# A hand-written list scheduler is given new costs: measured occupancies, a first-come port, banks chosen by the plan, single score and value tiles

## The chip, the cores and the metric

The kernel runs on one core of one Trainium2 chip. The metric is the device time of one execution in microseconds. A core has five engines with queues of their own: PE (matmuls; the profile shows its weight loads as PEld), DVE (VectorE), ACT (ScalarE), POOL (GpSimd) and SP (SyncE, here only for DMAs). Each runs its own instructions strictly in the order in which the program issues them, and waits on semaphores for the others.

## The reference

Sixteen graphs (batches) of 1024 nodes with 256 features go through two layers; the same 0/1 adjacency masks both.

```python
def _L0_gnn_ref(features, adj, Wq, Wk, Wv, Wffn, g1, b1, g2, b2):
    q, k, v = heads(features @ Wq), heads(features @ Wk), heads(features @ Wv)   # 8 heads of 32
    e = jnp.einsum('whqd,whkd->whqk', q, k)
    e = jnp.where(e >= 0, e, ALPHA * e)
    attn = jax.nn.softmax(jnp.where(adj[:, None] > 0, e, NEG), axis=-1)
    h = jnp.einsum('whqk,whkd->whqd', attn, v)
    ...
    out = _layernorm(h, g1, b1)
    out = jnp.concatenate([out, features], axis=-1) @ Wffn.T
    return _layernorm(out, g2, b2) + features

def _gat(h, adj, W, a, out_features):                                            # twice in layer 1
    Wh = jnp.matmul(h, W)
    e = leaky_relu(Wh @ a[:out_features] + swapaxes(Wh @ a[out_features:], 1, 2))
    att = jax.nn.softmax(jnp.where(adj > 0, e, NEG), axis=1)
    return jnp.matmul(att, Wh)
...
    h = _layernorm(residual + _gat(_gat(x, ...), ...), g_ln1, b_ln1)
    ff = relu(h @ w_ff1 + b_ff1) @ w_ff2 + b_ff2                                 # 256 -> 1024 -> 256
    return _layernorm(h + ff, g_ln2, b_ln2)
```

## The kernel before

For each batch b the work has three kinds of parts, and parts of neighbouring batches run beside each other.

**Preparing batch b+1** (`project`): x is loaded and transposed (L355), the adjacency is turned into an 8-bit mask by DVE (L412), transposed (L422) and copied (L426); q and k of two groups of four heads are made as products L475, which ACT copies out rounded (L478, "high") and DVE as the remainder (L480, "low"); both go to DRAM and come back stacked for each head (L568). The values are products L507, copied out at L514 or L516.

**The heads** (`all_scores`, `weights`, `all_values`): for each of 8 heads and 8 key tiles, two matmuls (L601) make a 128 x 1024 score tile in two PSUM banks. ACT scales it (L619), DVE takes the maximum (L621) and so frees the score banks, ACT takes the exponential (L624), POOL multiplies with the mask (L628). The result p, one of five buffers, is multiplied with the values (L650), two halves of 512 columns beside each other on 33 (or 64) columns of the array. For b > 0 the score matmuls of two key tiles are issued together and both score tiles are taken first; the value matmuls of two key tiles (GV = 2) are always issued as one group, after which both p are given back.

**The rest of batch b** (`rest`): normalisations, the projection (L753, L756), rows of the first graph layer (L785), the attention matrix of 8 tiles on DVE (L838, L841), its product with the rows (L876), the second layer's attention and product (L901, with residual by L929), and the feed-forward part (L941, L969).

PSUM has eight banks: four for two score tiles, one for the values' sum, and three for all other products ("misc", `ps_m`). The misc tiles have one tag with three buffers, so the framework hands the banks out in rotation; a product waits for the one made three before it.

**The order** of all instructions is made when the kernel is built, by class `Order` (L35 to L175). Every part above is a generator. It yields `on(ENGINE=cost, ...)` before it issues an instruction, `take` and `give` for buffers, `wait` and `fire` for data, and `aim` for the time at which it should run. `run` keeps a clock for each engine and issues, among those that could start at most WINDOW = 300 ns after the earliest, the one with the lowest aim. A cost with two engines goes to the one that ends first. An operation marked `shared` on DVE or POOL also waits for the common SBUF port. After an operation the thread is ready HOP later (60 to 100 ns), except on the same engine. Matmuls run at half speed in the plan in a stretch of 3413 ns after one that was less than 43% busy. The plan's pools are counted, not numbered: it takes whichever misc bank is free first. Aims are shares of SLOT = 253 us after a batch's start; the constants are in `AIM` (batches from 2 on) and `EARLY` (0 and 1). None of the costs is read by the chip; only the order of the instructions, and which of two engines does a copy, come out of them.

Of the kernel before, what the change touches and what calls it, by code (L numbers as in the profile page):

```python
# [34 lines left out]
class Order:  # L35
# [5 lines left out]

    HOP = dict(PE=100.0, ACT=70.0, DVE=60.0, POOL=70.0, SP=60.0)
    WINDOW = 300.0

# [3 lines left out]
    def __init__(self, **pools):  # L54
        self.clock = defaultdict(float)
        self.port = 0.0
        self.transfers = 0.0
        self.stretch, self.done, self.half = 0, 0.0, True
        self.pools = {k: [0.0] * n for k, n in pools.items()}
        self.queues = defaultdict(list)  # L60
        self.events = {}
        self.waiting = defaultdict(list)
        self.active = []
        self.made = 0
        self.now = 0.0
        self.busy = defaultdict(float)

    def add(self, thread, aim, ready=0.0):
        self.made += 1
        self.step({"gen": thread, "aim": aim, "no": self.made, "ready": ready}, None)  # L70

    def step(self, th, sent):
        while True:
# [19 lines left out]
            elif what == "take":  # L93
                if not self.pools[arg]:
                    self.queues[arg].append(th)
                    return
                th["ready"] = max(th["ready"], self.pools[arg].pop(0))
            elif what == "give":
                queue = self.queues[arg]
                if queue:  # L100
                    other = min(queue, key=lambda o: (o["aim"], o["no"]))
                    queue.remove(other)
                    other["ready"] = max(other["ready"], th["ready"])
                    self.step(other, None)
                else:
                    self.pools[arg].append(th["ready"])
                    self.pools[arg].sort()
            elif what == "start":
                self.add(arg[0], arg[1], th["ready"])
            elif what == "pause":  # L110
                th["ready"] += arg
            elif what == "aim":
                th["aim"] = arg[0]
                th["ready"] = max(th["ready"], arg[0] - arg[1])
# [19 lines left out]
    def run(self):  # L134
        while self.active:
            could = []
            for th in self.active:
                costs, shared, delay = th["op"]
                best = None
                for engine, cost in costs.items():  # L140
                    ready = th["ready"]
                    if th.get("last", ())[:2] == (engine, ready):
                        ready -= self.HOP[engine]
                    t = max(self.clock[engine], ready)
                    if shared and engine in ("DVE", "POOL"):
                        t = max(t, self.port)
                    if best is None or t + cost < best[0] + best[2]:
                        best = t, engine, cost
                could.append((best, th))
            first = min(c[0][0] for c in could)  # L150
            (t, engine, cost), th = min((c for c in could if c[0][0] <= first + self.WINDOW),
                                        key=lambda c: (c[1]["aim"], c[1]["no"]))
            if th["op"][1] and engine in ("DVE", "POOL"):

                lead = 100.0 if engine == "DVE" else -100.0
                before = [c for c in could if c[1]["op"][1] and c[0][1] in ("DVE", "POOL")
                          and c[0][1] != engine and c[0][0] + lead < t]
                if before:
                    (t, engine, cost), th = min(before, key=lambda c: (c[1]["aim"], c[1]["no"]))
            costs, shared, delay = th["op"]  # L160
            self.active.remove(th)
            end = self.clock[engine] = self.end(engine, t, cost)
# [4 lines left out]
            th["ready"] = end + self.HOP[engine]  # L167
# [10 lines left out]
def on(shared=False, delay=0.0, **costs):  # L178
    return "on", (costs, shared, delay)
# [45 lines left out]
def unshifted_path(  # L225
# [28 lines left out]
    AIM = dict(mask0=0.759, x=0.818, x_step=0, mask=0.747, mask_step=0.0264, qk0=0.614, qk1=0.898,  # L254
               qk_step=0.0231, v0=0.832, v1=0.974, v_step=0.0591, rows=-0.244, rows_step=0.0408, first0=0.12,
               first1=0.252, graph0=-0.009, graph1=0.21, graph_step=0, second=0.355, second_step=0.0335,
               normed=0.78, normed_step=0.026, ff_wait=(None, 0, 1, 0), ff=(0.532, -0.011, 0.487, 0.497),
               ff_step=0.0386, fast0=0.425, fast1=0.938, fast15=0.832, lead=3.15)

    EARLY = dict(x=0.87, x_step=0.005, mask=0.747, mask_step=0.0296, qk0=0.692, qk1=0.909, qk_step=0.0345,  # L260
                 v0=0.774, v1=1.001, v_step=0.0568, rows=-0.139, rows_step=0.0071, first0=0.082, first1=-0.169,
                 graph0=-0.195, graph1=-0.027, graph_step=0, second=0.302, second_step=0.0335, normed=0.781,
# [14 lines left out]
    def misc(dtype=FT):  # L277
        return psum.tile([P, HALF], dtype, tag="misc", name="ps_m", bufs=bufs["misc"])
# [36 lines left out]
    def evacuate(n):  # L315
        return on(DVE=140 + 1.06 * n, ACT=150 + 0.87 * n)

    def evacuate_by(n):

        return on(DVE=190 + 1.06 * n, ACT=250 + 0.87 * n)  # L320
# [5 lines left out]
    def stats(srcs):  # L326
# [3 lines left out]
        for i, src in enumerate(srcs):  # L330
            st = small.tile([P, 6], FT, name="st")
            yield on(DVE=420)
            nc.vector.bn_stats(st, src)
            yield on(DVE=185)
            nc.vector.bn_aggr(mv[:, i, :], st)  # L335
        rs = small.tile([P, n], FT, name=f"rs{n}")
        yield on(POOL=260)
        nc.gpsimd.tensor_scalar(rs, mv[:, :, 1], EPS, None, op0=OP.add)  # L338
        yield on(POOL=450 + 150 * n, shared=True)
# [3 lines left out]
    def normalized(dst, srcs, mv, rs):  # L343
        for i, (row, src) in enumerate(zip(dst, srcs)):
            if row is src:
                yield on(DVE=340, shared=True)
            else:
                yield on(DVE=440)
# [38 lines left out]
    def mask_part(b, t, halves):  # L387
# [22 lines left out]
        for i, ai in enumerate(ints):  # L410
            yield on(DVE=440, shared=True)
# [8 lines left out]
        yield on(PE=90 + 112 * n)  # L420
# [3 lines left out]
        yield on(ACT=150 + 225 * n)  # L424
# [19 lines left out]
    def x_pair(b, u):  # L444
# [7 lines left out]
        yield on(PE=450)  # L452
# [7 lines left out]
    def qk_part(b, g, o, nh):  # L460
# [12 lines left out]
        yield on(PE=1720)  # L473
# [3 lines left out]
        yield on(ACT=590)  # L477
        nc.scalar.copy(high.bitcast(FR), pa)  # L478
        yield on(DVE=690)
# [20 lines left out]
    def v_part(b, g, u):  # L500
# [3 lines left out]
        yield on(PE=1000)  # L504
# [15 lines left out]
    def project_v(b, g, t0):  # L520
# [3 lines left out]
        yield on(POOL=500)  # L524
# [56 lines left out]
    def all_scores():  # L581
        for b in range(B):
# [4 lines left out]
            for h in range(H):  # L587
                yield wait(("stack", b, h))
                q, kk = stacks[b, h]
                n = 2 if b else 1  # L590
                for t in range(0, NT, n):
                    due = t0 + (h * NT + t) / 2 * pace(b)
                    yield aim(due, AIM["lead"] * PACE)
                    for _ in range(n):
                        yield take("scores")
                    ps = [psum.tile([P, N], FT, tag="scores", name="ps_s") for _ in range(n)]
                    yield on(PE=450 * n)
                    for i in range(n):
                        for nh in range(NH):
                            cols = slice(nh * HALF, (nh + 1) * HALF)  # L600
                            nc.tensor.matmul(ps[i][:, cols], kk[:, (t + i) * P:(t + i + 1) * P], q[:, cols],  # L601
                                             start=True, stop=True)
                    if t + n == NT:
                        yield give("stacks")
                    for i in range(n):
                        yield start(weights(b, h, t + i, ps[i]), due + i * PACE / 2)

    def weights(b, h, t, ps):
# [3 lines left out]
        if b == 0:  # L612
            engine = yield on(ACT=1050, DVE=1230)
        else:
            engine = yield on(ACT=1050)
# [4 lines left out]
        yield on(DVE=1220)  # L620
        nc.vector.tensor_tensor(p, p, ps, op=OP.max)  # L621
        yield give("scores")
        yield on(ACT=1080)
# [3 lines left out]
        yield on(POOL=2050, shared=True)  # L627
# [3 lines left out]
    def all_values():  # L631
        for b in range(B):
            for h in range(H):
# [6 lines left out]
                for d in range(0, NT, GV):  # L640
                    for t in range(d, d + GV):
                        yield wait(("p", b, h, t))
                    yield aim(begin[b] + (h * NT + d + 2) / 2 * pace(b), SLOT)
                    yield on(PE=240 + 860 * GV)
                    for t in range(d, d + GV):
                        p = probs.pop((b, h, t))
                        for nh in range(NH):

                            m = VW if t else 64
                            nc.tensor.matmul(acc[nh * 64:nh * 64 + m, :], v[:, t, c:c + m],  # L650
                                             p[:, nh * HALF:(nh + 1) * HALF],
                                             start=(t == 0), stop=(t == NT - 1))
                    for t in range(GV):
                        yield give("p")
# [5 lines left out]
    def after_head(b, h, acc):  # L660
# [14 lines left out]
        yield on(PE=450)  # L675
# [5 lines left out]
        yield on(DVE=210)  # L681
        nc.vector.reciprocal(rd, src[:, :, :, DH])
        yield on(DVE=430)
# [20 lines left out]
    def add_b2(b, u):  # L704
        for dc in range(DC):
            part = xTs[b][:, dc, 2 * u * P:2 * (u + 1) * P]
            yield on(ACT=480)
# [18 lines left out]
    def rows_pair(b, u):  # L726
# [12 lines left out]
        yield on(PE=450)  # L739
# [10 lines left out]
        for i, t in enumerate(tiles):  # L750
            yield on(PE=1720)
# [14 lines left out]
        yield on(PE=450)  # L766
# [4 lines left out]
        for dc in range(DC):  # L771
            yield on(DVE=470)
# [6 lines left out]
        for t in tiles:  # L779
# [7 lines left out]
            yield on(ACT=380)  # L787
            nc.scalar.copy(y1[:, t, :], pa[:, :YW])
            yield on(DVE=180)
# [21 lines left out]
    def first_half(b, s, nh):  # L811
# [7 lines left out]
        yield on(PE=600)  # L819
        for i in range(TPH):  # L820
            nc.tensor.transpose(pt[:, i * P:(i + 1) * P], ac[:, nh * TPH + i, 0:1].to_broadcast([P, P]), ident)
        yield on(ACT=600)
        nc.scalar.activation(first[:, 0, cols], pt, AF.Exp)
        yield on(ACT=600)
# [4 lines left out]
    def attend(b, s, big, rows, j, second, sums):  # L829
# [7 lines left out]
        yield on(DVE=1270, shared=True)  # L837
        nc.vector.scalar_tensor_tensor(e, first[:, 0, :], second[:, j:j + 1], first[:, 1, :],  # L838
                                       op0=OP.mult, op1=OP.max)
        yield on(DVE=1250, shared=True)  # L840
        nc.vector.scalar_tensor_tensor(e, mask_of(b, j), -1.0, e, op0=OP.mult, op1=OP.mult,  # L841
                                       accum_out=sums[:, j:j + 1])
        yield on(DVE=160)
        nc.vector.reciprocal(den, sums[:, j:j + 1])  # L844
        yield on(ACT=510)
# [3 lines left out]
    def attention(b, s, rows, at):  # L849
# [8 lines left out]
        yield on(ACT=220)  # L858
# [13 lines left out]
    def products(pa, cols, big, rows, i, width):  # L872
        for half in range(2):
            yield on(PE=6.68 * width)
# [4 lines left out]
    def second_rows(b, big, y1, y2, i):  # L879
# [3 lines left out]
        yield on(ACT=380)  # L883
        nc.scalar.copy(y2[:, i, :], pa[:, :YW])
        yield on(DVE=180)
# [4 lines left out]
    def normed_pair(b, u, big, y2):  # L890
# [6 lines left out]
        for i, t in enumerate(tiles):  # L897
            for half in range(2):
                yield on(PE=1720)
# [3 lines left out]
            yield on(PE=430)  # L903
# [10 lines left out]
        yield on(PE=450)  # L914
# [17 lines left out]
    def hidden(hid, rT, hp, done):  # L932
# [4 lines left out]
        yield on(PE=1720)  # L937
# [5 lines left out]
        for i in range(2):  # L943
            hc = 2 * hp + i
            engine = yield on(DVE=470, ACT=470)
# [9 lines left out]
    def feed_forward(b, u, rT):  # L955
# [9 lines left out]
        for i in range(2):  # L965
            for half in range(2):
                yield on(PE=1720)
# [3 lines left out]
            yield on(PE=430)  # L971
# [6 lines left out]
        for i, (row, src) in enumerate(zip(rows, srcs)):  # L978
            yield on(DVE=490, shared=True)
            nc.vector.scalar_tensor_tensor(row, src, mv[:, i, 0:1], k["gl2"], op0=OP.subtract, op1=OP.mult)  # L980
            yield on(DVE=490, shared=True)
# [55 lines left out]
    def prepare():  # L1037
# [80 lines left out]
        yield on(PE=3000)  # L1118
# [23 lines left out]
    pa = misc()  # L1142
# [303 lines left out]
```

## Time and profile before

| | us |
|---|---|
| median of 3 runs | 4487.69 (4481.99 to 4490.15) |
| profiled execution: span, first to last instruction | 4479.9 |
| PE busy | 4325.9 |
| DVE busy | 3311.9 |
| ACT busy | 2887.7 |
| POOL busy | 2474.9 |
| DMA moved | 343.57 MB |

The page gives no time of the profiled execution but its span. Busy time of an engine is the union of its instructions' spans; PE's include the modelled drain of a matmul, so that two matmuls in a row overlap in the trace. Idle time of an engine is put down to what released the instruction after it. DMA-issuing and waiting instructions aren't busy time. In the lines, L650 is line 650 of the kernel, `ps_a<-p,v` names what is written and read, and x4 counts instructions.

### The profile page before, as it was taken

To read this page: it belongs to the slowest core of one execution; us is meant where nothing else is said; L and a number is where in the kernel's file an instruction comes from. 1 tells how busy PE (TensorE), PEld (TensorE's weight loads), DVE (VectorE), ACT (ScalarE), POOL (GpSimd) and SP (SyncE) were. 2 spreads that over 40 slices of the span, in tenths; PEclk is the share of its full clock that TensorE was granted. 3 is DMA by queue.
4 is the path that set the end of the run, shared out by engine and by line. 5 is a ranking of instruction groups with operands and counts; after the bars stand their busy time and mean duration, and the time that the engine had idled before them with its cause. 6 is when DMAs were issued, how large, how long until landed. Compare 5 with 4: busy or idle time off the path is not lost.

```text
span 4479.9 us, 57088 instructions
## 1 busy us (share of the span) xinstructions
PE 4325.9 (97%) x20299; PEld 2866.3 (64%) x20299; DVE 3311.9 (74%) x5263; ACT 2887.7 (64%) x4015; POOL 2474.9 (55%) x1544
## 2 busy tenths in 40 slices
PE   8888999999999999999999999999999999999998
PEld 3444656667666675766667666676666667666587
DVE  6877867687776877778777776877778777776754
ACT  6666675666667666666666666666666666666631
POOL 5756565554565556556554565546556554665610
PEclk9989999999999999999999999999999999999999
DMA  6423222232232313223231232323223231232100
GB/s 187 114 66 87 66 73 77 73 92 73 68 88 63 107 59 86 76 59 99 64 106 55 74 96 62 103 63 80 80 64 99 64 102 55 71 92 55 27 22 20
DMA packets 156209, 343.57 MB, mean 77 GB/s; under 512 B 21751, under 2 KB 24333, under 8 KB 155917
## 3 DMA queue, kind: packets, MB, share of 16 engines
q1 hardware_dynamic: 112140, 260.13, 20.8%
q10 hardware_dynamic: 43776, 79.71, 6.1%
q8 instruction: 164, 2.69, 0.3%
q14 instruction: 129, 1.05, 0.1%
HBM read 239.09 MB, written 100.66 MB: 76 GB/s over the span
## 4 chain that ended last, share of the span: by engine, by line
PE 69%; DVE 18%; issue 5%; POOL 5%; ACT 2%; DMA 0%; POOLq 0%; ACTq 0%; DVEq 0%
PE ps_a L650 16%; PE ps_s L601 9%; PE ps_m L901 8%; PE ps_m L876 8%; PE ps_m L941 7%; PE ps_m L969 6%; DVE att L841 5%; DVE att L838 5%; POOL p L628 4%; DVE p L621 4%; PE ps_m L785 3%; PE ps_m L475 3%; PE ps_m L753 2%; PE ps_m L756 2%; PE ps_m L355 2%
## 5 line engine op out<-in xcount | busy, mean ns | idle before, releaser
L628 POOL TENSOR_TENSOR p<-p,mask 128x1024 f32<-128x1024 f32 x1024 | 2232.2, 2197 | 1564.6 <-ACT p L624 1444.7
L621 DVE TENSOR_TENSOR p<-p,ps_s 128x1024 f32<-128x1024 f32 x1024 | 1211.1, 1214 | 399.3 <-ACT p L619 397.8
L624 ACT ACTIVATE p<-p 128x1024 f32<-128x1024 f32 x1024 | 1080.9, 1058 | 377.5 <-DVE p L621 355.7
L619 ACT ACTIVATE p<-ps_s 128x1024 f32<-128x1024 f32 x995 | 974.9, 1025 | 186.7 <-PE ps_s L601 172.1
L650 PE MATMUL ps_a<-p,v 128*33 128x512 f32 (+1 forms) x4096 | 1000.6, 606 | 24.2 <-POOL p L628 22.9
L601 PE MATMUL ps_s<-qs,ks 128*128 128x512 f32 x2048 | 634.5, 428 | 39.2 <-DVE p L621 38.3
L601 PEld LDWEIGHTS ps_s<-qs,ks 128*128 128x128 f32 x2048 | 349.5, 190 | 343.2 <-DVE p L621 106.2
L650 PEld LDWEIGHTS ps_a<-p,v 128*33 128x33 f32 (+1 forms) x4096 | 199.7, 114 | 531.3 <-issue 405.3
L901 PE MATMUL ps_m<-y,att 128*128 128x256 f32 x2048 | 480.5, 380 | 12.7 <-ACT v L516 11.0
L941 PE MATMUL ps_m<-rT,wf 128*128 128x256 f32 x2048 | 479.8, 384 | 10.7 <-ACT z L313 3.6
L969 PE MATMUL ps_m<-wf,hid 128*128 128x256 f32 x2048 | 475.1, 381 | 10.6 <-ACT xT L313 8.9
L876 PE MATMUL ps_m<-y,att 128*128 128x258 f32 x2048 | 472.4, 381 | 0.0
L969 PEld LDWEIGHTS ps_m<-wf,hid 128*128 128x128 f32 x2048 | 379.4, 190 | 78.6 <-issue 14.8
L876 PEld LDWEIGHTS ps_m<-y,att 128*128 128x128 f32 x2048 | 385.2, 189 | 63.6 <-issue 3.3
L901 PEld LDWEIGHTS ps_m<-y,att 128*128 128x128 f32 x2048 | 375.0, 189 | 77.3 <-ACT v L516 13.1
L941 PEld LDWEIGHTS ps_m<-rT,wf 128*128 128x128 f32 x2048 | 380.9, 192 | 63.4 <-ACT z L313 3.8
L838 DVE SCALAR_TENSOR_TENSOR att<-first,second 128x1024 f32<-128x1024 f32 x256 | 354.4, 1384 | 73.2 <-ACT first L825 73.2
L841 DVE SCALAR_TENSOR_TENSOR att<-mask,att 128x1024 f32<-128x1024 fp8e4 x256 | 352.0, 1375 | 8.7
L846 ACT ACTIVATE y<-y,check 128x258 f32<-128x258 f32 x256 | 130.9, 511 | 305.3 <-DVE check L844 278.4
L338 POOL TENSOR_SCALAR rs<-mv 128x2 f32<-128x2 f32 (+1 forms) x224 | 60.0, 268 | 410.9 <-DVE mv L335 410.8
L412 DVE TENSOR_SCALAR adj_b<-adj_i 128x512 fp8e4<-128x512 int32 x256 | 234.0, 958 | 14.8 <-DMA adj_i<-in_adj_dram 9.3
L950 ACT ACTIVATE hid<-ps_m,columns 128x256 f32<-128x256 f32 x372 | 159.2, 472 | 119.8 <-PE ps_m L941 94.3
(105 smaller groups left out, 4232.5 us busy)
## 6 DMA issues: line engine op xcount, KB each, us to landing
qs<-qk_halves SPq DMA_DIRECT2D x256, 256.0 KB, 4.2
ks<-qk_halves SPq DMA_DIRECT2D x256, 256.0 KB, 5.1
adj_i<-in_adj_dram ACTq DMA_DIRECT2D x240, 256.0 KB, 3.5
qk_halves<-high SPq DMA_DIRECT2D x128, 256.0 KB, 2.4
qk_halves<-low SPq DMA_DIRECT2D x128, 256.0 KB, 3.6
xr<-in_x_dram ACTq DMA_DIRECT2D x64, 256.0 KB, 3.1
x_kept<-x SPq DMA_DIRECT2D x64, 256.0 KB, 4.8
x<-x_kept SPq DMA_DIRECT2D x64, 256.0 KB, 6.8
```

The lines of the kernel that those rows point to most:

```text
L601: nc.tensor.matmul(ps[i][:, cols], kk[:, (t + i) * P:(t + i + 1) * P], q[:, cols], start=True, stop=True)
L619: nc.scalar.activation(p, ps, AF.Copy, scale=ALPHA)
L621: nc.vector.tensor_tensor(p, p, ps, op=OP.max)
L624: nc.scalar.activation(p, p, AF.Exp)
L628: nc.gpsimd.tensor_tensor(p, p, mask_of(b, t), op=OP.mult)
L650: nc.tensor.matmul(acc[nh * 64:nh * 64 + m, :], v[:, t, c:c + m], p[:, nh * HALF:(nh + 1) * HALF], start=(t == 0), stop=(t == NT - 1))
L838: nc.vector.scalar_tensor_tensor(e, first[:, 0, :], second[:, j:j + 1], first[:, 1, :], op0=OP.mult, op1=OP.max)
L841: nc.vector.scalar_tensor_tensor(e, mask_of(b, j), -1.0, e, op0=OP.mult, op1=OP.mult, accum_out=sums[:, j:j + 1])
L876: nc.tensor.matmul(pa[:, cols:cols + width], big[:, j, i * P:(i + 1) * P], rows[:, j, :width], start=(j == 0), stop=(j == NT - 1))
L901: nc.tensor.matmul(pa[:, i * D:(i + 1) * D], big[:, j, t * P:(t + 1) * P], y2[:, j, :D], start=(j == 0), stop=False)
L941: nc.tensor.matmul(pa[:, i * 2 * P:(i + 1) * 2 * P], wf1[:, dc, hc * P:(hc + 1) * P], rT[:, dc, :], start=(dc == 0), stop=(dc == DC - 1))
L969: nc.tensor.matmul(pa[:, i * D:(i + 1) * D], hid[hc // 2][:, hc % 2, i * P:(i + 1) * P], wf2[:, hc, :], start=(hc == 0), stop=False)
```

## The change

The planner's class, its costs and two emission loops are changed. No instruction's operands change but for the bank that a product is put into, and for what engine a copy falls to by the plan; the same matmuls are made.

```diff
-    HOP = dict(PE=100.0, ACT=70.0, DVE=60.0, POOL=70.0, SP=60.0)
+    HOP = dict(PE=53.0, ACT=35.0, DVE=36.0, POOL=80.0, SP=60.0)
+    TAIL = dict(PE=163.0, ACT=103.0, DVE=84.0, POOL=42.0, SP=0.0)
     WINDOW = 300.0
+    SWITCH = 93.0
...
-                    ready = th["ready"]
-                    if th.get("last", ())[:2] == (engine, ready):
-                        ready -= self.HOP[engine]
-                    t = max(self.clock[engine], ready)
+                    ready = th["ready"] + self.HOP[engine]
+                    if th.get("last", ())[:2] == (engine, th["ready"]):
+                        ready -= self.HOP[engine] + self.TAIL[engine]
+                    t = asked = max(self.clock[engine], ready)
...
-                lead = 100.0 if engine == "DVE" else -100.0
                 before = [c for c in could if c[1]["op"][1] and c[0][1] in ("DVE", "POOL")
-                          and c[0][1] != engine and c[0][0] + lead < t]
+                          and c[0][1] != engine and c[0][3] < asked]
...
+            if engine == "PE":
+                if narrow != self.narrow:
+                    cost += self.SWITCH
+                self.narrow = narrow
...
-            th["ready"] = end + self.HOP[engine]
+            th["ready"] = end + self.TAIL[engine]
...
     def misc(dtype=FT):
-        return psum.tile([P, HALF], dtype, tag="misc", name="ps_m", bufs=bufs["misc"])
+        return psum.tile([P, HALF], dtype, tag=f"misc{work.slot['misc']}", name="ps_m", bufs=1)
```

So an operation that asks for the port later than another engine's doesn't go ahead of it, a hand-over costs the first engine's TAIL and the second one's HOP, a change between value matmuls ("narrow") and others costs PE 93 ns, and each of the three misc banks is a tag of its own, which the plan numbers (`taken` keeps the slot; the pool is sorted by the time at which a slot comes free).

```diff
-                n = 2 if b else 1
-                for t in range(0, NT, n):
+                for t in range(NT):
                     due = t0 + (h * NT + t) / 2 * pace(b)
                     yield aim(due, AIM["lead"] * PACE)
-                    for _ in range(n):
-                        yield take("scores")
-                    ps = [psum.tile([P, N], FT, tag="scores", name="ps_s") for _ in range(n)]
-                    yield on(PE=450 * n)
+                    yield take("scores")
+                    ps = psum.tile([P, N], FT, tag="scores", name="ps_s")
+                    yield on(PE=471)
...
-                for d in range(0, NT, GV):
-                    for t in range(d, d + GV):
-                        yield wait(("p", b, h, t))
-                    yield aim(begin[b] + (h * NT + d + 2) / 2 * pace(b), SLOT)
-                    yield on(PE=240 + 860 * GV)
...
-                    for t in range(GV):
-                        yield give("p")
+                for t in range(NT):
+                    yield wait(("p", b, h, t))
+                    if t % GV == 0:
+                        for other in range(t + 1, t + GV):
+                            yield wait(("p", b, h, other))
+                        yield aim(begin[b] + (h * NT + t + 2) / 2 * pace(b), SLOT)
+                    else:
+                        yield aim(begin[b], BIG)
+                    yield on(PE=860, narrow=True)
...
+                    yield give("p")
```

The costs, some of many, and the aims:

```diff
-        return on(DVE=140 + 1.06 * n, ACT=150 + 0.87 * n)
+        return on(DVE=66 + 1.06 * n, ACT=45 + 0.855 * n)
...
-        yield on(ACT=590)
+        yield on(ACT=466)
         nc.scalar.copy(high.bitcast(FR), pa)
-        yield on(DVE=690)
+        yield on(DVE=594)
         nc.vector.tensor_tensor(low, pa, high, op=OP.subtract)
...
-        yield on(PE=1000)
+        yield on(PE=880)
...
-            engine = yield on(ACT=1050)
+            engine = yield on(ACT=910)
...
-        yield on(DVE=1220)
+        yield on(DVE=1130)
         nc.vector.tensor_tensor(p, p, ps, op=OP.max)
         yield give("scores")
-        yield on(ACT=1080)
+        yield on(ACT=962)
         nc.scalar.activation(p, p, AF.Exp)
...
-        yield on(POOL=2050, shared=True)
+        yield on(POOL=2098, shared=True)
...
-        yield on(PE=600)
+        yield on(PE=437)
...
-            yield on(PE=430)
+            yield on(PE=218)
             as_rows(pa, i, x1, i)
...
-    AIM = dict(mask0=0.759, x=0.818, x_step=0, mask=0.747, mask_step=0.0264, qk0=0.614, qk1=0.898,
...
-               graph0=-0.009, graph1=0.21, graph_step=0, second=0.355, second_step=0.0335,
-               normed=0.78, normed_step=0.026, ff_wait=(None, 0, 1, 0), ff=(0.532, -0.011, 0.487, 0.497),
-               ff_step=0.0386, fast0=0.425, fast1=0.938, fast15=0.832, lead=3.15)
+    AIM = dict(mask0=0.759, x=0.818, x_step=0, mask=0.747, mask_step=0.0264, qk0=0.614, qk1=0.7723, qk_step=0.0231,
...
+               graph0=-0.0093, graph1=0.1976, graph_step=0, second=0.355, second_step=0.0335, normed=0.78,
+               normed_step=0.058, ff_wait=(None, 0, 1, 0), ff=(0.532, 0.0483, 0.487, 0.497), ff_step=0.0561,
+               fast0=0.4247, fast1=0.938, fast15=0.8086, lead=3.2293)
```

Some steps of `EARLY` move in the third decimal place.

## The prediction

> **What bounds the kernel now.** I read the page first, then the long stretches one under the other, then PE's waits in one of the stretches that repeat, then the order of time around the largest of those waits.
>
> ```profile
> span 4479.9 us, 57088 instructions
> ...
> PE 4325.9 (97%) x20299; PEld 2866.3 (64%) x20299; DVE 3311.9 (74%) x5263; ACT 2887.7 (64%) x4015; POOL 2474.9 (55%) x1544
> ...
> PEclk9989999999999999999999999999999999999999
> ```
>
> PE is busy 97% of the span, the next engine 74%, and the granted clock is near full except at the start. A busy PE is not a dense PE, so I take starts instead of ends below. The stretches (us, then busy time of PE, PEld, DVE, ACT, POOL, the clock and the DMA) say where PE is thin:
>
> ```profile
> 13.20:283.30 270.10, 232.96 (x999) 113.54 (x997) 218.34 (x275) 175.55 (x240) 178.57 (x94) 0.91 0.44 124
> 283.30:553.50 270.20, 244.51 (x1106) 152.70 (x1104) 197.97 (x300) 169.69 (x225) 163.37 (x90) 0.96 0.28 78
> 823.60:1093.70 270.10, 262.99 (x1246) 173.60 (x1245) 207.94 (x333) 177.30 (x242) 153.02 (x96) 1.00 0.27 78
> 2174.30:2444.40 270.10, 266.29 (x1266) 177.75 (x1265) 204.02 (x326) 182.36 (x254) 152.73 (x96) 1.00 0.28 79
> 4065.30:4480.00 414.70, 387.00 (x1811) 293.05 (x1809) 253.61 (x468) 180.19 (x280) 140.45 (x103) 0.99 0.10 29
> ```
>
> From 1094 us on the kernel repeats itself every 270.14 us, 11 times, until 4065 us: in the chain of work the same 32 matmuls of L941 start at 1093.74, 1363.91, 1634.05 and so on. One such period holds one batch.
>
> How dense it is I get from the start-to-start distances of the matmuls in the order of time. Inside a group they are steady: 216 ns for 256 columns (L901, L941, L969, L753, L756), 217 and 219 for 258 and 260, 235 for a score matmul (L601), 429 for L475, 112 for L507, 109 for a transpose, 430 for a pair of value matmuls (L650, the two run beside each other). The value matmuls (33 or 64 columns of the array) cost more at both ends: the last matmul before them takes 309 where 216 is usual, and their own last one 523 where 430 is usual, so 93 ns a change and 64 changes a period. Summed over the 1264 to 1266 matmuls of a period this gives 260.0 us, and 270.1 - 260.0 = 9.9 us are lost (rounded as the starts give it). Over the whole run the same sum is 4168 us, with 298 lost of the 4466 from first to last matmul: about 80 before 283 us, 41, 20 and 14 in the next three stretches, 11 x 9.9 = 109 in the repeated ones, 29 after 4065 us. That, and nothing else, is what an order can win: it removes no arithmetic.
>
> What the 9.9 are, by PE's waits in the period 2174.34 to 2444.49:
>
> ```profile
> PE ps_m L901 <- ACT v L516: 1.0, 1, 1.0
> PE ps_a L650 <- POOL p L628: 0.9, 2, 0.8
> PE ps_m L969 <- ACT xT L313: 0.7, 1, 0.7
> PE ps_m L507 <- ACT v L516: 0.5, 1, 0.5
> PE ps_m L677 <- ACT ho L313: 0.5, 1, 0.5
> PE ps_m L475 <- DVE low L480: 0.2, 1, 0.2
> ```
>
> By starts these seven waits cost 1.17, 0.93 + 0.33, 0.89, 0.68, 0.61 and 0.33: 4.94 us. Some 4 more are the first matmuls after a value group, which come late once more (336 instead of 235 ns for a score, 50 to 105 ns for others, 26 inside the group), at 32 groups; the rest is small. So **about 5 us of 270 can be won by a better order**, and 4 only by fewer value groups.
>
> Four of the seven are waits for a product bank. The largest, in order of time:
>
> ```profile
> 2272.77 1.88 PE L475 MATMUL ps_m<-xT,wq 128*128 128x512 f32 x4
> ...
> 2281.83 1.88 PE L475 MATMUL ps_m<-xT,wk 128*128 128x512 f32 x4
> ...
> 2284.69 0.39 ACT L516 ACTIVATE v<-ps_m 128x256 f32<-128x256 f32 x1
> ...
> 2285.13 1.16 PE L507 MATMUL ps_m<-wv,xT 128*128 128x128 f32 x8 [0.52 <-ACT v L516]
> ...
> 2286.87 0.37 ACT L516 ACTIVATE v<-ps_m 128x256 f32<-128x256 f32 x1
> 2287.29 1.99 PE L901 MATMUL ps_m<-y,att 128*128 128x256 f32 x8 [1.00 <-ACT v L516]
> ...
> 2289.61 0.66 DVE L480 TENSOR_TENSOR low<-ps_m,high 128x512 f32<-128x512 f32 x1
> ```
>
> Two q/k products are done by 2273 and 2284 us, but DVE reaches their L480 only at 2289.61, because the attention pairs L838 and L841 stand before it. Two of three banks are parked for that time, and everything else goes through the third.
>
> **The change, part by part.**
>
> *Banks chosen by the plan.* It matters only where the bank that rotation hands out is held while another is free. I laid each product's first matmul against the end of its last reader: at each of the four bank waits of the period all three banks were held (two q/k products and one more), and likewise at the bank waits over 0.6 us of the first 1094 us. So by itself this is worth nothing here: 0, with ends of 0 and -0.6 us a period (a fifth of the four waits' 3.07). The Trainium skill, "Perfetto Trace Analysis", section Matmuls, speaks against it: independent matmul groups should rotate through the banks so that the evacuation lies beside the next group. By that rule a bank taken again at once would cost the evacuation each time. No row here shows such a loss, since the plan takes the bank that came free first, which is nearly the rotation; I keep 0.
>
> *Scores one tile at a time.* Today both score tiles are taken before the first matmul (n = 2). The matmuls are the same 128 a period. A score group enters without a loss from any group but the values (28 ns, then 419 after a four-pass product: 447 against 216 + 235), so twice as many groups cost 0 on PE as long as the value groups stay 32. What they can save is small too, since no score wait over 0.2 us is left in the period; in the head, "PE ps_s L601 <- DVE p" waits are 38.3 us in all, and that is batch 0, which takes single tiles already. Value 0, ends -1 and +1 us a period.
>
> *Values one tile at a time.* The first tile still waits for both, and the second gets the aim begin[b], which goes ahead of nearly all. So the pair stays together; its p buffer is only given back 0.86 us earlier. A pair that is split costs 93 + 93 for the changes, 26 and about 100 for the late first matmuls: 0.31 us. Only operations with an aim before begin[b] (rows of the batch before, aimed at 0.244 SLOT before its end) can get in between: at most a few pairs, +1 us. I take 0.
>
> *Costs, hand-overs, port, aims: the new order.* The old plan took too much for some of what it orders: 1000 for the eight L507 that take 896, 430 for the two L929 that take 218, 600 for L821's four that take 436. The rows of ACT and DVE get shorter too in the new plan, and the hand-overs longer (60 to 100 ns before; TAIL and HOP together 120 to 216 now). The new numbers are near the rows, so its idea of when a bank comes free should be too. The port rule follows: the DVE operations L982 take 485 ns at least and 2355 at most, the long ones beside L628. First come is what these rows look like. And q/k of the second group is aimed 0.126 SLOT earlier, 32 us, which moves the parked products away from where they collide now, to an unknown place. Bounds: all seven waits gone, -4.94 a period; or a pattern like the stretch before 1094 us, which loses 14.2 against 9.9, +4.3 a period. I take half of the seven waits, -2.5, because costs that are off can explain each of the seven (a bank or a p that comes later than planned), but each new order parks products somewhere. 11 x -2.5 = **-27 us** (ends -54, +47).
>
> *Head (to 1094 us).* 155 lost there, of which 4 x 5 are floor. Batch 0 is held by POOL and DVE (178.6 and 218.3 of the first 270 us are busy) and by a clock of 0.91, which an order touches only indirectly; the EARLY aims hardly move. A tenth of the 135: **-14 us** (ends -60, +30).
>
> *Tail (after 4065 us).* 29 lost, 8 of it floor; the last batch's scores are paced 3% faster. **-3 us** (ends -15, +15).
>
> Sum: -27 - 14 - 3 = -44 against the span of 4479.9: 4436. The page gives the profiled execution's span alone; the runs' median lies 7.8 us above it, so 4436 + 7.8 = **4443.5 us**.
>
> **The rivals.** (A) The replanned order loses what it lost before: the collision moves, nothing else. For it: the bank waits are scarcity, not a wrong bank. 4480 to 4497. (B) The plan now sees the chip as it is, and nearly all waits go: -54 - 45 - 10 = -109, 4379. For it: the period is exact, so one good order is won 11 times. (C) Slower: more q/k products parked. DVE and ACT look shorter to the new plan, so it may put more beside the attention pairs, and a period loses 14.2 as the one before 1094 us does (its waits are of this kind: two q/k products held and a third). +4.3 x 11 = +47, with the head unchanged: 4535. It decides once parked banks cost over 1.3 us more a period than the 3.07 now, since the head's -14 is then spent. (D) Value pairs get split: 0.31 each, 9.9 a period if all are, 8 of 32 eat the 2.5; at 16 a period 4443 + 55 = 4498.
>
> **How the numbers follow.** Forecast, faster by 0.2 to 1.9%: 0.55. B: 0.14. A: 0.11. C: 0.14. D: 0.06. About 0.2% (9 us) is what this kernel's runs can tell from no change. Faster 0.69, same 0.11, slower 0.20. Two in ten are left out by 4385 below (most of B) and 4525 above (the worse half of C and D).
>
> **What would show it.** Right: a repeated period of 266 to 269 us with 60 to 64 changes to and from the values, bank waits of L507, L901 and L969 halved, L480 sooner after L475. The bank choice is worth more than I say if after the change PE waits for a bank while none is parked by q/k any more. Wrong: a period over 270.2; over 70 changes a period (D); L480 still 8 to 17 us after its product (A, C); or a head that moves by more than 30 us either way, which I can't derive from its rows.

## The result and the profile after

| us | before | after |
|---|---|---|
| median (7 runs each) | 4485.8 (4481.99 to 4490.15) | 4498.52 (4497.39 to 4503.39) |
| profiled execution, its span | 4479.9 | 4501.6 |
| start of batch 4's scores | 1024.3 | 1003.4 |
| start of batch 15's scores | 3995.8 | 4023.1 |
| a repeated period (after: from batch 10 on) | 270.1 | 273.1 |

The changed kernel is slower: 1.0031 times the time before [1.002, 1.0041]. The forecast was 4443.5, so faster; the time lies inside the range that was given, but the kernel moved the other way. The profiled execution of after took 4503.39, 1.8 more than its span, and is the slowest of the seven. The spans differ by 21.7: the head (up to batch 4's scores) gave 20.9, the eleven batches after it took 48.2, and the rest gave 5.6. Of the 48.2, batch 4 alone took 12.1 (282.3 us); batches 5 to 9 take 273.6 to 274.9, the later ones 273.1.

A part of these three numbers is work that moved, not time lost. Counted by starts, as in the prediction, the matmuls ahead of batch 4's scores take 14.1 us less of PE's time in the changed kernel, because fewer of them stand there; 9.5 of that is done in the eleven batches instead and 4.6 in the rest. Without it the head is 6.5 better, the eleven batches are 38.7 worse, and the rest is 10.0 better.

The page of the changed kernel, and its stretches (columns as in the prediction; the fifth is one of its repeated periods, the last the tail):

```profile
span 4501.6 us, 57032 instructions
...
PE 4340.4 (96%) x20299; PEld 2860.2 (64%) x20299; DVE 3221.4 (72%) x5299; ACT 2863.3 (64%) x3979; POOL 2603.0 (58%) x1544
...
PEclk9999999999999999999999999999999999999999
```

```profile
13.20:283.30 270.10, 228.08 (x1002) 115.10 (x1002) 201.57 (x282) 178.10 (x246) 170.29 (x93) 0.95 0.43 126
283.30:553.50 270.20, 250.81 (x1151) 153.69 (x1148) 186.40 (x295) 179.19 (x238) 175.00 (x95) 0.99 0.28 78
553.50:823.60 270.10, 256.80 (x1189) 164.22 (x1188) 194.40 (x316) 175.66 (x234) 170.00 (x97) 0.98 0.25 73
823.60:1093.70 270.10, 263.73 (x1229) 172.40 (x1229) 197.81 (x336) 179.18 (x246) 156.02 (x96) 0.99 0.28 80
...
2957.70:3230.80 273.10, 267.88 (x1266) 177.57 (x1265) 200.28 (x330) 179.66 (x250) 164.14 (x97) 1.00 0.27 78
4051.20:4501.60 450.40, 433.68 (x2032) 325.51 (x2032) 262.96 (x504) 216.61 (x345) 173.93 (x122) 0.99 0.11 32
```

PE has the same instructions and DVE is less busy, but a period of the same 1266 matmuls takes 3 us more. POOL is 128 us busier; its 1024 products with the mask take 2308 ns each where they took 2197, by the groups of the page. The second stretch holds 45 more matmuls than before (1151 against 1106), but the first four together only 7 more (4571 against 4564): the changed kernel reaches its later batches sooner in part by putting other work off.

PE's waits in that period:

```profile
PE ps_s L604 <- DVE p L622: 2.4, 3, 1.1
PE ps_m L972 <- DVE low L486: 1.0, 1, 1.0
PE ps_m L879 <- ACT hid L953: 0.6, 1, 0.6
PE ps_m L944 <- ACT v L522: 0.5, 1, 0.5
PE ps_m L361 <- DVE hid L950: 0.4, 1, 0.4
PE ps_m L481 <- DVE hn L687: 0.3, 1, 0.3
```

(L604 is the score matmul, L601 before; L622 the maximum, L629 the mask product, L841 and L844 the attention matrix, L486 "low", L522 the copy of v.) The two waits of the value matmuls for p are gone, and a wait for v at 0.5 is left of three. In their place PE waits three times for a score bank. By starts: 6.4 us of waits a period against 4.9.

The same accounting by starts for the whole run, first to last matmul. "Late" is everything lost in pieces up to 200 ns, the first matmuls in and behind the value groups above all:

| us | dense, with 93 ns a change | late | waits for a bank or data / a score bank / p | changes |
|---|---|---|---|---|
| before | 4168 | 98 | 108 / 53 / 40 | 1024 |
| after | 4173 | 115 | 94 / 81 / 25 | 1084 |

The waits are 200 in both: what was won at the product banks and at p was lost at the score banks. Over the whole run the 22 us are thus 5 for 60 more changes to and from the values and 17 more of the small pieces: about 6 at the value groups, of which there are 30 more (0.2 us each), about 6 at score matmuls that come directly behind some other product (431 where there were 240), the rest scattered. In the eleven batches alone the waits do grow, from 54 to 73 us, the small pieces by 14 to 15, and the changes cost 4.5 more: these are the 38.7.

One score wait in order of time:

```profile
3115.56 3.12 POOL L629 TENSOR_TENSOR p<-p,mask 128x1024 f32<-128x1024 f32 x1
...
3119.23 8.27 POOL L629 TENSOR_TENSOR p<-p,mask 128x1024 f32<-128x1024 f32 x3 [0.55 <-ACT p L625]
...
3122.47 3.04 DVE L844 SCALAR_TENSOR_TENSOR att<-mask,att 128x1024 f32<-128x1024 fp8e4 x1
...
3123.18 1.91 PE L654 MATMUL ps_a<-p,v 128*33 128x512 f32 x8
...
3125.03 0.73 PE L604 MATMUL ps_s<-qs,ks 128*128 128x512 f32 x2
...
3125.63 1.20 DVE L622 TENSOR_TENSOR p<-p,ps_s 128x1024 f32<-128x1024 f32 x1
...
3126.89 0.74 PE L604 MATMUL ps_s<-qs,ks 128*128 128x512 f32 x2 [1.13 <-DVE p L622]
```

While POOL runs three products back to back, L844 takes 3.04 us, where 1.21 to 1.23 is usual in this trace with POOL idle. L622 stands behind it in DVE's queue and frees the score bank only at 3126.83. On PE the next single tile is already the head of the queue, so everything after it waits 1.13 us as well. The Trainium skill ("SBUF — State Buffer", section "Who interferes with whom") says that the port pair which DVE and GpSimd share is an exclusive lock; the 3.04 beside 1.21 agrees with it.

### The profile page after: what moved, and what is told of

Its sections match the earlier page's. It is cut to its first block, busy times and chain, and to the rows that moved or that the text cites. A ratio compares the mean times of both kernels' runs of the same rounds, so it can differ in the third digit from the quotient of the medians.

```text
span 4501.6 us, 57032 instructions
## 1 busy us (share of the span) xinstructions
PE 4340.4 (96%) x20299; PEld 2860.2 (64%) x20299; DVE 3221.4 (72%) x5299; ACT 2863.3 (64%) x3979; POOL 2603.0 (58%) x1544
## 5 line engine op out<-in xcount | busy, mean ns | idle before, releaser
L629 POOL TENSOR_TENSOR p<-p,mask 128x1024 f32<-128x1024 f32 x1024 | 2344.1, 2308 | 909.7 <-ACT p L625 791.8
L622 DVE TENSOR_TENSOR p<-p,ps_s 128x1024 f32<-128x1024 f32 x1024 | 1222.8, 1214 | 453.8 <-ACT p L620 449.8
L620 ACT ACTIVATE p<-ps_s 128x1024 f32<-128x1024 f32 x997 | 994.0, 1024 | 198.2 <-PE ps_s L604 157.7
L604 PE MATMUL ps_s<-qs,ks 128*128 128x512 f32 x2048 | 692.8, 440 | 66.2 <-DVE p L622 64.5
L604 PEld LDWEIGHTS ps_s<-qs,ks 128*128 128x128 f32 x2048 | 338.1, 190 | 377.6 <-DVE p L622 135.9
L841 DVE SCALAR_TENSOR_TENSOR att<-first,second 128x1024 f32<-128x1024 f32 x256 | 418.7, 1636 | 10.5 <-ACT first L828 10.3
L844 DVE SCALAR_TENSOR_TENSOR att<-mask,att 128x1024 f32<-128x1024 fp8e4 x256 | 401.1, 1567 | 4.7
L319 ACT COPY y<-ps_m 128x512 f32<-128x512 f32 x108 | 63.3, 586 | 265.5 <-PE ps_m L932 160.7
```

Source lines behind the costliest of these rows:

```text
L604: nc.tensor.matmul(ps[:, cols], kk[:, t * P:(t + 1) * P], q[:, cols], start=True, stop=True)
L620: nc.scalar.activation(p, ps, AF.Copy, scale=ALPHA)
L629: nc.gpsimd.tensor_tensor(p, p, mask_of(b, t), op=OP.mult)
```

## The experiments

In all of these kernels but e3 and e4 the computation is whole. "The plan's clock" is the time at which the planner's own last operation ends: 4459.8 before (by the old costs), 4425.0 after. So the plan promised 34.8 us, and the chip lost 12.7.

### Banks numbered by the framework, and by the plan in the old order

```diff
 after:   return psum.tile([P, HALF], dtype, tag=f"misc{work.slot['misc']}", name="ps_m", bufs=1)
 e1:      return psum.tile([P, HALF], dtype, tag="misc", name="ps_m", bufs=bufs["misc"])
 before -> e2: the reverse, with the plan's slots; the order of the instructions stays that of before
```

> The changed kernel with one line undone: the three product banks are one tag with three buffers again, as before the change, so that the framework picks the bank. The order of all instructions stays that of the changed kernel. Theory 1 (the order itself is worse, the banks are worth nothing): 4492 to 4505 us, a repeated period of 273.1 us within 0.3. Theory 2 (the plan's banks cost what was lost): at most 4488 us, a period of 270 to 271.

> The kernel before with the banks numbered by its own plan; its order is unchanged. Theory 1: 4480 to 4491 us, a period of 270.1 within 0.3. Theory 2: over 4495 us, a period of 272 or more. If the choice is worth something (the change's idea): under 4478.

e1 took 4500.75, 1.0044 of before [1.0027, 1.0061], not to be told from after (1.0031), as theory 1 said; its period did not stay within 0.3. In the later batches it is 274.2 against 273.1, with 7.4 us of waits by starts against 6.4, but all eleven batches together take only 3.1 more, and the head takes 4.2 less. e2 took 4560.43, 1.0177 [1.016, 1.0194], and its period is 276.5: in the old order the numbering does cost, which theory 1 denied. Where e2 loses, PE's waits in a period and the order of time:

```profile
PE ps_m L684 <- DVE check L893: 4.2, 1, 4.2
PE ps_m L684 <- DVE low L487: 1.6, 1, 1.6
```

```profile
2236.97 1.20 PE L608 MATMUL ps_s<-qs,ks 128*128 128x512 f32 x4
...
2242.41 0.88 PE L684 MATMUL ps_m<-ident,ho 97*128 97x97 f32 x4 [4.24 <-DVE check L893]
```

The plan thought the bank free when DVE had not read it yet (L893 reads it until 2242.26), and a fixed number can't be corrected on the chip: the last readers of the other two banks had ended at 2225.1 and 2231.4. So the numbering is only as good as the plan's clock. With the new costs it is worth nothing that shows; with the old ones it costs 6.4 us a period.

The runs also mend a sentence of mine: the kernel before does not hand its banks out in rotation, and so a product does not always wait for the one made three before it. In it, of 1560 steps from one product's bank to the next (in the order in which the program makes the tiles), 689 go one bank on, 686 two, and 185 stay. With the plan's numbers 347 stay, at no loss that shows between after and e1. The advice to rotate that the prediction names (the Trainium skill, "Perfetto Trace Analysis", section Matmuls) was no objection here.

### POOL's mask product on half the columns

```diff
-        nc.gpsimd.tensor_tensor(p, p, mask_of(b, t), op=OP.mult)
+        nc.gpsimd.tensor_tensor(p[:, :HALF], p[:, :HALF], mask_of(b, t)[:, :HALF], op=OP.mult)
```

> The changed kernel, in its own order, with POOL's product L629 on the first 512 of 1024 columns of p only: the second half is not masked. So POOL holds the common port half as long. Port theory (the new score waits come from DVE operations that L629 holds up): the waits for L622 of 2.9 us a period go, and the period falls from 273.1 by 2.5 to 4.5 us; the whole run by 35 to 70. Rival (the score tiles come too close together whatever the port does): the period stays within 1.2 us of 273.1.

> The kernel before, in its own order, with the same half of L628 left out. Port theory: less is to be had here, since its attention operations run where POOL is idle: the 1.3 us of waits for a late p go, some of the head, and the period falls from 270.1 by 1 to 2 us. Rival (any order gains alike from a shorter POOL): as much as the changed kernel gains.

Half of the weights go unmasked, in after (e3) and in before (e4). Their sums then fall outside what the kernel's own guard allows, so it runs its general path behind the fast one: 17801 and 17728 us in all. Only the first 4440 us are read, which hold the same order. The period falls to 270.9 in e3 (by 2.2, a little less than the 2.5 expected) and to 266.8 in e4 (by 3.3, where 1 to 2 were expected). PE's score wait in a period of e3:

```profile
PE ps_m L972 <- DVE low L486: 0.8, 1, 0.8
...
PE ps_s L604 <- DVE p L622: 0.4, 1, 0.4
```

So POOL holding the port does make two of the three score waits (2.91 to 0.56 by starts). But the old order gains more still from the same relief, and the new one remains 4.0 us a period behind. The port load is a cause of single waits, not what separates the two orders. e11 below shows the same from the other side: there 283 of the 512 attention instructions run beside a mask product, after 248 in the changed kernel and 86 before, and it is faster than both.

### One part of the change undone at a time

```diff
 e5 (from after):  AIM and EARLY of before
 e6 (from after):  n = 2 if b else 1 ... on(PE=471 * n); values: on(PE=860 * GV, narrow=True), p given after the group
 e7 (from after):  c[0][3] < asked   ->   lead = 100.0 if engine == "DVE" else -100.0; c[0][0] + lead < t
 e8 (from before): the new class and costs with before's port rule, emission and aims
```

> The changed kernel with the aims of the kernel before (AIM and EARLY). The planner's own clock, on which its last operation ends, is 4425.0 for the changed kernel, which took 4498.5 us, 73.5 more; for this one it ends at 4490.1. Theory 1 (the aims were fitted to this very plan; the chip follows the new clock but for an amount that it does not count and that is the same for all its plans): 4490 + 73 = 4563 us, within 20. Theory 3 (the parts add up, and the new aims are what is bad): below 4498, towards 4486.

> The changed kernel with scores taken by two key tiles for b > 0 and value matmuls as one operation of two tiles, as before (costs 942 and 1720, the value group marked narrow). The planner's clock ends at 4516.2. Theory 1: 4516 + 73 = 4589 us, within 20, with 64 changes to and from the values a period. Theory 3 (single tiles are what costs, by 2.9 us of score waits and four more changes a period): 4440 to 4470.

> The changed kernel with the old rule for the common port (a lead of 100 for DVE, compared with the port's wait included). The planner's clock ends at 4557.7. Theory 1: 4631 us, within 25. Theory 3 (the first-come rule is what costs): below 4498.

> The kernel before with the new costs alone (operations, HOP, TAIL, SWITCH): old aims, old port rule, pairs, banks by the framework. The planner's clock ends at 4506.6. Theory 1: 4580 us, within 20. Theory 3 (the better costs are what is good in the change): below 4480.

| | plan's clock | one run, us | above the clock |
|---|---|---|---|
| after | 4425.0 | 4498.5 | 73 |
| e5 old aims | 4490.1 | 4574.26 | 84 |
| e6 pairs | 4516.2 | 4520.28 | 4 |
| e7 old port | 4557.7 | 4751.21 | 193 |
| e8 costs alone | 4506.6 | 4659.85 | 153 |

The theory that the chip always takes 73 us more than the plan held for e5 only. e6 also falls against the rival that single scores alone made the loss: with pairs and otherwise everything of after, the kernel is not below 4470 but at 4520. No part can be judged by undoing it: each of the four is slower than both kernels, I think because the aims are fitted to one plan. For the port rule the distance gives a hint and no proof. With the new costs the plan is off by 153 and 193 us under the old rule and by 4 to 84 under first come; but the kernel before, with the old rule and its own costs, is only 26 us off (4459.8 against 4485.8).

### Counting the late first matmuls, and fitting the aims again

The plan charges 93 ns for every change. By starts, the first matmuls come late on top of it (means of the whole runs): 36 ns in a value group, 62 to 77 behind it, 95 to 98 if that is a score. So a change into the values costs some 93 + 36 = 129 ns, one out of them 155 to 191; e9 and e10 charge 119 and 185; e11 and e12 keep 93. In all four, the aims were fitted again to the plan's own clock by small random steps, once each; e10 and e12 take scores by pairs and were fitted from before's aims.

```diff
-    SWITCH = 93.0
+    INTO, OUT = 119.0, 185.0                             # e9, e10
...
-                    cost += self.SWITCH
+                    cost += self.INTO if narrow else self.OUT
...
-                for t in range(NT):                      # e10, e12
+                n = 2 if b else 1
+                for t in range(0, NT, n):
```

> The changed kernel, but PE's change into the value matmuls costs 119 in the plan instead of 93 (with 26 for the late second pair in the group) and the change out of them 185 (with some 92 for the late first matmul behind), and AIM and EARLY are fitted anew by small random steps that keep what ends sooner on this clock (from 4509 at the change's aims down to 4419). Theory 4 (the changed order lost what it won to some 130 ns a value group that its clock did not count, 70 us in all; with that counted, the clock and the chip agree within 15 us): 4415 to 4440 us. Rival (what a fitted order wins on any such clock is lost again on the chip, since the fit finds the clock's errors): 4470 or more.

> The same, with the scores taken by two key tiles for b > 0 as before the change; fitted from the old aims, to 4433 on that clock. The pairs' clock counts a wait for both score tiles ahead of the first matmul, which the chip has only ahead of the second, so that the run with pairs took 4 us more than its clock where single tiles took 73 more. Theory 4: 4433 less some 65, so 4360 to 4400 us, if that holds for a fitted order as well. Rival: 4470 or more.

> The changed kernel's planner, costs and single tiles as they are (SWITCH 93 both ways); AIM and EARLY are fitted on by as many small random steps as for the kernel with the late matmuls counted, from 4425.0 to 4400.5 on that clock. If single tiles keep the distance of the changed kernel between clock and chip (73 us): 4474 us, within 20. If the fall of the clock by 24.5 reaches the chip and the change's own aims were only badly met: the same 4474. If a fit on a clock with errors wins nothing: 4490 or more.

> The same without counting the late matmuls, but with scores by two key tiles for b > 0, fitted from the old aims to 4391.4 on the clock. If pairs keep their small distance (4 us in the run with pairs): 4395 us, within 15, so that taking the scores by pairs, and not the counting of the late matmuls, is what made the last version good. If the counting made it: 4391 + 70 = 4461 or more.

| | plan's clock | median, us (runs) | above the clock | ratio to before | period |
|---|---|---|---|---|---|
| e9 single, counted | 4419.4 | 4485.16 (10) | 66 | 0.9999 [0.999, 1.0009] | 272.9 |
| e10 pairs, counted | 4433.0 | 4410.61 (4) | -22 | 0.9838 [0.9822, 0.9854] | 268.1 |
| e11 single, 93 | 4400.5 | 4444.75 (4) | 44 | 0.9912 [0.9895, 0.9928] | 269.2 |
| e12 pairs, 93 | 4391.4 | 4418.37 (4) | 27 | 0.9853 [0.9837, 0.987] | 268.8 |

e10, e11 and e12 all lie outside every range that was expected of them: no rule for the distance between clock and chip held.

e9 makes the theory that the uncounted late matmuls are the cause fall: counted, the single tiles still miss 4415 to 4440. Of its 6.2 us of waits a period, by starts, 2.7 are for a score bank, and the largest single one (2.2) is for a product bank that L486 frees:

```profile
PE ps_s L604 <- DVE p L622: 2.4, 2, 1.7
PE ps_m L680 <- DVE low L486: 2.1, 1, 2.1
```

The larger of the two score waits comes from the port. In order of time, all engines:

```profile
2980.48 1.28 DVE L841 SCALAR_TENSOR_TENSOR att<-first,second 128x1024 f32<-128x1024 f32 x1
2980.56 13.55 POOL L629 TENSOR_TENSOR p<-p,mask 128x1024 f32<-128x1024 f32 x5
...
2989.01 3.11 DVE L841 SCALAR_TENSOR_TENSOR att<-first,second 128x1024 f32<-128x1024 f32 x1
...
2992.04 2.34 DVE L622 TENSOR_TENSOR p<-p,ps_s 128x1024 f32<-128x1024 f32 x2
...
2993.31 0.73 PE L604 MATMUL ps_s<-qs,ks 128*128 128x512 f32 x2 [1.69 <-DVE p L622]
```

In the plan the second L841 asks for the port 0.03 us before POOL's next product; on the chip that product starts 0.11 us before L841 by their records, so L841 takes 3.11 instead of 1.28, and PE waits 1.69. The plan's clock can't tell such near ties, and this one recurs in eight periods, from 1900 us on.

e11 settles more. It differs from after in the aims alone, and beats before by 0.9%. Single tiles, the new costs and rules, and banks numbered by the plan are in both, so it was none of these by itself that made the changed kernel slow, but the order that came out with its aims. Over the eleven batches e11's score waits are 0.2 us, against 30.6 in after, and all its waits 31 against 73 (54 before, 26 in e10). PE's waits in a period of it, then of e10, and e10's page:

```profile
PE ps_m L972 <- ACT xT L319: 0.8, 1, 0.8
PE ps_m L428 <- DVE hT L378: 0.4, 1, 0.4
PE ps_m L972 <- ACT v L522: 0.3, 1, 0.3
```

```profile
PE ps_m L977 <- ACT xT L319: 0.7, 1, 0.7
PE ps_m L949 <- ACT v L522: 0.5, 1, 0.5
PE ps_m L977 <- DVE hn L692: 0.4, 1, 0.4
```

```profile
span 4408.9 us, 56935 instructions
...
PE 4301.7 (98%) x20299; PEld 2859.4 (65%) x20299; DVE 3225.1 (73%) x5238; ACT 2904.3 (66%) x4040; POOL 2570.4 (58%) x1544
```

No score wait is left in either period. e10 is the fastest kernel of the study, 1.6% below before. It lies 8 us below e12, and the intervals overlap, so what counting the late matmuls brings for pairs does not show. Singles against pairs stays open too: one fit each, from different starts.

## Why the prediction was wrong

**The bound** held. The dense sum hardly moved (4168 to 4173, all of it changes), and the whole difference lies in what an order can win or lose. Two of the signs of success came. L480 (now L486) came sooner: over the eleven batches it starts 0.9 us after its "high" ends, where it took 2.7 (medians of 88). And the bank waits of L507, L901 and L969 fell from 30 to 11 us there. The period of 266 to 269 was not met, nor the 60 to 64 changes: 273.1 and 68.

**The new order, -2.5 a period ("half of the seven waits"), is the step that failed.** Its reason was right: the bank waits on v fell from 20.4 to 5.4 us over the eleven batches and the value waits from 13.7 to 0. But the step counted only the waits that go, and nothing that comes. Score waits came, 30.6 us where there were none, and the small losses rose by 14 (55.3 to 69.7). With 49 more changes (4.6) and what else waits, the eleven batches lost some 39 us more in place of 27 less; the other 9.5 of their 48.2 is work put off from the head.

**"Scores one tile at a time: value 0, ends -1 and +1"** is where the omission sits. I asked what singles could save, and found no score wait to save in a period. (That the 38.3 us of score waits are the head's and batch 0's was misread: 17.7 lie before 283 us, 10.5 until 1094, and 10.1 after 4065, where pairs are taken.) I did not ask who waits when a lone tile reaches the head of PE's queue while L622 stands behind a DVE instruction that POOL's mask product holds up (L844 above; before the wait at 3175.21 it is L355, a normalisation, at 4.28 us for two): 2.9 us a period, outside my ends. That it needed this particular order, and isn't a property of single tiles, e11 shows.

**"Values one tile at a time: value 0, at most a few pairs, +1"** was near: 2 of 32 pairs a period are split. The price was a little low: some 0.39 us (0.19 for two changes, 0.2 for late first matmuls) instead of 0.31.

**Banks by plan, 0 (ends 0 and -0.6)**: by e1 -3.1 us over the eleven batches, -0.3 a batch, and not to be told from 0 in the time. The argument by rotation was wrong, and that the same choice costs 6.4 a period in the old order (e2) was not in my ends. **Head -14**: it gave 20.9, but only 6.5 of that is time saved. At the start of batch 3's scores it was 48.9 ahead (703.3 against 752.2), with 36 us less of matmul work behind it, and gave 28 back in that batch. **Tail -3**: 5.6, and 10.0 without the work that moved into it.

Two more readings were off, at no cost to the sum. The first of the two parked products runs until 2274.65, not 2273. And a hand-over between two engines costs 77 (POOL to ACT) to 243 ns (PE to POOL) in the new plan; 120 to 216 are each engine's own two numbers added.

**The rivals.** C's 4535 had +47 for the eleven batches, and 48.2 came; yet its mechanism, more parked q/k products, did not happen, since those were parked for less time. The size was met by chance, and with 9.5 us of work that only moved. D's split pairs came as well, but 2 a period and not 16. The rival that should have stood there is a wait that takes the place of the ones removed, at the score banks.

**What stays open**: why the fit behind the changed kernel's aims ended where it did, and how often near ties fall badly; e9 to e12 are single draws.

## What to carry to other kernels

A change of a list scheduler is a new draw of the order as much as a better model: first ask which queue heads can now stand still (here a lone score tile behind a late maximum), and price the waits that come as well as those that go. Undoing parts one by one says little when due times were fitted to the whole; compare the plan's clock with the chip instead, and fit again under each model (e10 to e12 were 0.9 to 1.6% faster where after lost 0.3%; e9, the fourth fit, won nothing). Whatever is fixed at build time by the plan's clock, such as a bank's number, is only as good as that clock (e2).

## What was not expected of the hardware

A value group on part of the array costs more than its two changes of 93 ns: the late first matmuls at its ends add about 36 + 95 = 131 ns where a score follows. POOL's mask product takes 2.14 us alone and 3.12 where an attention instruction of 1.2 holds the port, and the attention instruction 3.04 to 3.11 the other way round: who asks first by 0.1 us decides 1.0 us on POOL and 1.8 on DVE.
